# A recommender's attention over 200 history positions: three of 128 tiles per position fetched row by row, two by SyncE and one by ScalarE, instead of four

## The chip, the cores and the metric

The kernel runs on one core of one Trainium2 chip. The metric is the device time of one execution in microseconds (us). Engines are named as in the profile: PE is TensorE (PEld its weight loads), DVE is VectorE, ACT is ScalarE, POOL is GpSimd and SP is SyncE; a name with q is the queue of DMA issues and control instructions of that engine.

## What is computed

Of the reference, this is what matters (B = 16,384 users, L = 200 history positions, D = 64 values in a row, tables of 100,000 rows for items and users):

```python
def dice(x, alpha, axis):
    mean = jnp.mean(x, axis=axis, keepdims=True)
    var = jnp.var(x, axis=axis, keepdims=True)
    p = jax.nn.sigmoid((x - mean) * jax.lax.rsqrt(var + EPS))
    return x * (p + alpha * (1.0 - p))

u = u_emb[user]
it = i_emb[item]
c = c_emb[cate]
h = i_emb[hist]                      # 200 x 16384 rows of 64
itb = jnp.broadcast_to(it[None], h.shape)
feat = jnp.concatenate([h, itb, h - itb, h * itb], axis=-1)
a = dice(feat @ au_W1 + au_b1, au_alpha, axis=1)
w = a @ au_W2 + au_b2
cur = jnp.sum(w * jax.lax.stop_gradient(h), axis=0)
z = jnp.concatenate([u, it, c, cur], axis=-1)
z = dice(z @ W1 + b1, alpha1, axis=0)
z = dice(z @ W2 + b2, alpha2, axis=0)
return z @ W3 + b3
```

For each history position l, 16,384 rows are fetched from the item table at random indices. A small layer of 36 hidden values runs on each, is normalised over the 16,384 users of that l, and gives one weight per row; the weighted rows are summed over l. A head of three layers follows once.

## The kernel before

**Tiles and steps.** A tile is 128 rows. One l has 128 tiles, cut into eight chunks (c = 0 to 7) of sixteen tiles. One chunk is one step k (c = k % 8, l = k // 8), and there are 1,600 steps. Positions 0 to 179 run in a hardware loop of four passes of 45 l (LPB, line 19); the last 20 l and the head are written out behind it. The order of the instructions on each engine is written by hand, in `step` (line 368).

**Fetching.** `fetch` (304) writes the sixteen tiles of a chunk into one of five row buffers (128 x 16 x 64). POOL does it with one indirect DMA per tile (`gather`, 124; the call is line 125): 128 row indices lie in SBUF, one per partition, and each picks a row of 256 bytes. Chunks in SIDES = (1, 3, 5, 7) have only fifteen gathers; their sixteenth tile comes "by address". For it the indices, times the row length, lie as a list of integers in one partition (`load_addresses`, `scale_addresses`); an engine loads eight or sixteen of them into registers and issues one plain DMA of 256 bytes for each row (`addresses`, 267). For chunks 1 and 5 SP issues these (`rows_by_sync`, 275, asked for by `ask`, 398, 32 rows in each step), into one of three `side` buffers. For chunks 3 and 7 ACT issues them (`rows_by_scalar`, 285, in groups of eight, four groups in each step, split by `scalar_rows`, 403, into two slots of the step), into one of three `aside` buffers, with a semaphore for each (`landed`) on which ACT itself waits (`await_rows_by_scalar`, 295) for all 128 rows.

**One step, engine by engine.** The numbers are lags: step k fetches chunk k, transposes chunk k - 1, finishes the hidden layer of chunk k - 2 and weighs chunk k - 10, whose l has its mean and variance by then.

- `gate(k - 10)` (310): ACT writes p = sigmoid of the normalised hidden values into PSUM (pg).
- `weights(k - 10)` (314): DVE multiplies pg by the hidden values x into y; PE sums over the hidden values into wb, as blk_x times x plus blk_p times y. blk_x holds alpha times W2, blk_p holds (1 - alpha) times W2.
- `scalar_rows` slot 0, then `hidden(k - 2)` (322, ACT: px plus bias into x), `measure(k - 2)` (325, DVE: statistics of x), then `scalar_rows` slot 1.
- `turn(k - 1)` (330): in chunks of SIDES, ACT copies the tile that came by address into the row buffer (line 339); DVE transposes the buffer into hT (four instructions, line 154); PE multiplies hT by a unit matrix into ph in PSUM, and then begins px with blk_h times hT and blk_i times the item values.
- `weigh(k - 10)` (318, DVE): the weights times hT of chunk k - 10, added to the running sums.
- `product(k - 1)` (344): DVE multiplies ph by the item values into hm; PE adds blk_m times hm to px.
- `moments` (348), once per l: mean, variance, scale and shift; ACT takes a square root (168).

All matmuls but the head's second layer go through one helper, so they stand at line 159.

Of the kernel before, what the change touches and what calls it, by code (L numbers as in the profile page):

```python
# [9 lines left out]
I32 = mybir.dt.int32  # L10
AF = mybir.ActivationFunctionType
ALU = mybir.AluOpType
PSUM = bass.MemoryType.PSUM

P = 128
# [3 lines left out]
S = 32  # L19
CD = 2 * CH  # L20
LPB = 45
ROWS = 5
LAG = 10
XR = 9
IDX = 3
BY_SP = (1, 5)
BY_ACT = (3, 7)
SIDES = (1, 3, 5, 7)
LOAD = 16
GROUP = 8  # L30
ROW = 4 * D
U8 = mybir.dt.uint8
# [3 lines left out]
def din_kernel(  # L36
# [24 lines left out]
    nc = tc.nc  # L61
    L, B = r_hist.shape
    NT = B // P
    TD = 2 * CD // P
    ND = NT // TD
# [3 lines left out]
    ZA = P // 2  # L69
    ZB = Z1 - ZA  # L70
    NS = len(SIDES)
    NB, NA = len(BY_SP), len(BY_ACT)
    serial = iter(range(10**6))
    NC = NT - NS
    BODY = L - L % LPB if L > LPB else 0
    STATS = nc.vector.BN_STATS_DIM
# [5 lines left out]
    def make(name, *shape, dt=F32):  # L82
        return const.tile(list(shape), dt, name=name)
# [4 lines left out]
    def quarter(e, g, n=S):  # L88
        return slice((2 * e + g) * S, (2 * e + g) * S + n)
# [11 lines left out]
    ph = psum.tile([P, CD], F32, name="ph")  # L101
    pg = psum.tile([P, CD], F32, name="pg")
    wb = psum.tile([P, CD], F32, name="wb")

    rows = [make(f"rows{i}", P, TD, D) for i in range(ROWS)]
    hT = [make(f"hT{i}", P, CD) for i in range(LAG)]
    xs = [make(f"xs{i}", P, CD) for i in range(XR)]
# [3 lines left out]
    y = make("y", P, CD)  # L111
# [3 lines left out]
    side = [make(f"side{i}", P, D) for i in range(3)]  # L115
    aside = [make(f"aside{i}", P, D) for i in range(3)]
    landed = [tc.alloc_semaphore(f"landed{i}") for i in range(3)]
    addrs = make("addrs", 2 * S + 1, NS * P, dt=I32)
    addr = [addrs[i * S : i * S + 1] for i in range(3)]
    stats = [make(f"st{i}", P, 2 * ND, STATS) for i in range(3)]  # L120
    rstds = [make(f"rs{i}", P, 1) for i in range(3)]
    shifts = [make(f"sh{i}", P, 1) for i in range(3)]
# [33 lines left out]
    def layer(dst, pairs, first=True, last=True):  # L156
        for i in range(2):
            for j, (lhsT, rhs) in enumerate(pairs):
                nc.tensor.matmul(  # L159
                    dst[:, ts(i, CH)], lhsT, rhs[:, ts(i, CH)],  # L160
                    start=(first and j == 0), stop=(last and j == len(pairs) - 1),
                    skip_group_check=not (first and last),
                )
# [9 lines left out]
    blk_h = make("blk_h", P, P)  # L173
    blk_i = make("blk_i", P, P)
    blk_m = make("blk_m", P, P)
    blk_p = make("blk_p", P, P)
    blk_x = make("blk_x", P, P)
    unit = make("unit", P, P)
    au_w = make("au_w", P, 4, A)
    au_bias = make("au_bias", P, 1)  # L180
    au_al = make("au_al", P, 1)
# [4 lines left out]

    def attention_weights():
        nc.vector.memset(eps, EPS)
        for t in (blk_h, blk_i, blk_m, blk_p, au_bias, au_al, au_w2):
            nc.vector.memset(t, 0.0)  # L190
        nc.sync.dma_start(au_bias2, au_b2.partition_broadcast(P))
        for e in range(2):
            w = au_W1.rearrange("(g d) a -> d g a", d=D)[e * S : (e + 1) * S]
            for g in range(2):
                r = quarter(e, g)
                nc.sync.dma_start(au_w[r], w)
                for q, (a0, n) in enumerate(halves):
                    c, a = quarter(q, g, n), slice(a0, a0 + n)
                    nc.vector.tensor_add(blk_h[r, c], au_w[r, 0, a], au_w[r, 2, a])
                    nc.vector.tensor_sub(blk_i[r, c], au_w[r, 1, a], au_w[r, 2, a])  # L200
                    nc.vector.tensor_copy(blk_m[r, c], au_w[r, 3, a])
                    nc.vector.memset(blk_p[r, quarter(q, g)], 1.0)
        for g in range(2):
            for q, (a0, n) in enumerate(halves):
                r, a = quarter(q, g, n), slice(a0, a0 + n)
                nc.sync.dma_start(au_bias[r], col(au_b1)[a])
                nc.sync.dma_start(au_al[r], col(au_alpha)[a])
                nc.sync.dma_start(au_w2[r], au_W2[a])
        nc.vector.tensor_scalar(au_1al, au_al, -1.0, 1.0, ALU.mult, ALU.add)
        nc.vector.tensor_mul(au_1al, au_1al, au_w2)  # L210
        nc.vector.tensor_mul(au_al, au_al, au_w2)
        nc.vector.tensor_scalar_mul(blk_x, blk_p, au_al)
        nc.vector.tensor_scalar_mul(blk_p, blk_p, au_1al)
        nc.vector.tensor_copy(unit, lanes)
        nc.vector.tensor_single_scalar(unit, unit, float(P), ALU.is_equal)


    w1a = make("w1a", P, 4, P)
# [56 lines left out]
    def rows_by_sync(m, part, n):  # L275
        l, j = divmod(m, NB)
        s, dst = SIDES.index(BY_SP[j]), side[m % 3].bitcast(U8)
        for p0 in range(part * n, part * n + n, LOAD):
            for j, row in enumerate(addresses(l, s, p0, LOAD, mybir.EngineType.SP)):
                nc.sync.dma_start(dst[p0 + j : p0 + j + 1], row)  # L280


    keys = {}

    def rows_by_scalar(m, part):
        l, j = divmod(m, NA)
        s, dst = SIDES.index(BY_ACT[j]), aside[m % 3].bitcast(U8)
        key = keys.setdefault(m, f"rows{next(serial)}")
        for j, row in enumerate(addresses(l, s, part * GROUP, GROUP, mybir.EngineType.Activation)):
            p = part * GROUP + j  # L290
            dma = nc.scalar.dma_start(dst[p : p + 1], row).then_inc(landed[m % 3], 16)  # L291
            tc.no_tile_sem_insts.add(dma.ins.name)
            tc.add_to_no_dep_group(key, dma.ins)

    def await_rows_by_scalar(m):
        if m in keys:
            fence = nc.scalar.wait_ge(landed[m % 3], 16 * P)
            tc.declare_fence(fence.ins, group=keys.pop(m))
            nc.scalar.sem_clear(landed[m % 3])

    def has_side(k):
        return k % ND in SIDES
# [7 lines left out]
    def gate(k):  # L310
        i = k // ND % 3
        nc.scalar.activation(pg, xs[k % XR], AF.Sigmoid, bias=shifts[i], scale=rstds[i])  # L312

    def weights(k):
        nc.vector.tensor_mul(y, pg, xs[k % XR])  # L315
        layer(wb, [(blk_x, xs[k % XR]), (blk_p, y)])

    def weigh(k):
        nc.vector.scalar_tensor_tensor(wb, wb, au_bias2, hT[k % LAG], ALU.add, ALU.mult)  # L319
# [10 lines left out]
    def turn(k):  # L330
        if has_side(k):
            l, c = divmod(k, ND)
            if c in BY_ACT:
                m = l * NA + BY_ACT.index(c)
                await_rows_by_scalar(m)
                of = aside[m % 3]
            else:
                of = side[(l * NB + BY_SP.index(c)) % 3]
            nc.scalar.copy(rows[k % ROWS][:, TD - 1], of)  # L339
        transpose(hT[k % LAG], rows[k % ROWS])  # L340
        layer(ph, [(unit, hT[k % LAG])])
        layer(px, [(blk_h, hT[k % LAG]), (blk_i, itT[k % ND])], last=False)

    def product(k):
        nc.vector.tensor_mul(hm, ph, itT[k % ND])  # L345
# [47 lines left out]

    AHEAD = ND // NB - 1 - BY_SP[0]

    def ask(k, end):
        m, part = divmod(k + 1 + AHEAD, ND // NB)
        if m < end * NB:  # L400
            rows_by_sync(m, part, P * NB // ND)

    def scalar_rows(k, slot):
        m, part = divmod(k, ND // NA)
        n = P * NA // ND // GROUP
        for i in range(n)[slot::2]:
            rows_by_scalar(m, part * n + i)

    def steps(l0, n, end):
        for k in range(n * ND):  # L410
# [10 lines left out]
    with tc.manual_schedule():  # L421
        load_ids(ids[0], r_item)
        load_hist_ids(0, 0)
        load_addresses(0, 0)
        load_ids(ids[1], r_cate)
        load_ids(ids[2], r_user)
        nc.gpsimd.iota(lanes, pattern=[[1, P]], base=P, channel_multiplier=-1)
        attention_weights()
        for t in (*hT, *xs, *side, *aside, hm):
            nc.vector.memset(t, 0.0)  # L430
        for t in curT:
            nc.vector.memset(t, 0.0)
        for i in range(3):
            nc.vector.memset(rstds[i], 0.0)
            nc.vector.memset(shifts[i], 0.0)
        nc.vector.bn_stats(stats[-1 % 3][:, 0, :], hm[:, :CH])
        for c in range(1, 2 * ND):
            nc.vector.tensor_copy(stats[-1 % 3][:, c, :], stats[-1 % 3][:, 0, :])
        scale_addresses(0)
        layer(px, [(blk_m, hm)])  # L440

        for c in range(ND + 1):
            if c < ND:
                for n in range(TD):
                    j = column(c, n)
                    gather(rows[c % ROWS], ids[0][:, j : j + 1], n, i_emb)
            if c:
                transpose(itT[c - 1], rows[(c - 1) % ROWS])
        nc.vector.memset(rows[-1 % ROWS], 0.0)
        for k in range(-1 - AHEAD, 0):  # L450
            ask(k, L)
        head_weights()

    if BODY:
        with tc.For_i(0, BODY, LPB) as l0:  # L455
            with tc.manual_schedule():
                steps(l0, LPB, LPB + 1)
                await_rows_by_scalar(LPB * NA - 1)

    K = (L - BODY) * ND  # L460
    za = [hT[(K - LAG + c) % LAG] for c in range(ND)]
# [140 lines left out]
```

## Time and profile before

| | us |
|---|---|
| three executions | 31,616.96, 31,644.94, 31,647.4 |
| median | 31,644.94 |
| the profiled execution | 31,616.96 |
| its span, first to last instruction | 31,615.1 |
| mean granted TensorE clock | 0.810 |
| instructions | 357,535 |

The span is what the profile's shares refer to; the execution's own time is 1.9 us longer. In the profile's groups, a row gives line, engine, operation, output and inputs, the count, the busy time with the mean duration in ns, and the idle time of the engine just before, with what ended most of it. In a timeline, a row gives start, duration, engine, line, operation and, in brackets, the idle time before and what ended it; "issue" means that the engine waited for nothing that the profile shows. DMA issues and register work are not counted as busy.

### The profile page before, as it was taken

To read this page: it belongs to the slowest core of one execution; us is meant where nothing else is said; L and a number is where in the kernel's file an instruction comes from. 1 tells how busy PE (TensorE), PEld (TensorE's weight loads), DVE (VectorE), ACT (ScalarE), POOL (GpSimd) and SP (SyncE) were. 2 spreads that over 40 slices of the span, in tenths; PEclk is the share of its full clock that TensorE was granted. 3 is DMA by queue.
4 is the path that set the end of the run, shared out by engine and by line. 5 is a ranking of instruction groups with operands and counts; after the bars stand their busy time and mean duration, and the time that the engine had idled before them with its cause. 6 is when DMAs were issued, how large, how long until landed. Compare 5 with 4: busy or idle time off the path is not lost. (4 is left out here: it accounts for less than half of the span.)

```text
span 31615.1 us, 357535 instructions
## 1 busy us (share of the span) xinstructions
PE 20448.2 (65%) x38864; PEld 8357.2 (26%) x38864; DVE 15015.4 (47%) x18963; ACT 4479.6 (14%) x4670; POOL 23766.1 (75%) x25189
## 2 busy tenths in 40 slices
PE   5666666666666666666666666666666666666666
PEld 2222222222222222222222222222222222222222
DVE  4444444444444444444444444444444444444443
ACT  1111111111111111111111111111111111111111
POOL 7777777777777777777777777777777777777776
PEclk7888888888888888888888888888888888888887
DMA  1111111111111111111111111111111111111111
GB/s 29 28 28 28 28 28 28 28 28 28 28 28 28 28 28 28 28 28 28 28 28 28 28 28 28 28 28 28 28 28 28 28 28 28 28 28 28 28 28 23
DMA packets 1050292, 890.26 MB, mean 28 GB/s; under 512 B 644640, under 2 KB 644640, under 8 KB 1047784
## 3 DMA queue, kind: packets, MB, share of 16 engines
q0 software_dynamic: 805888, 826.84, 11.8%
q1 hardware_dynamic: 138920, 27.05, 0.4%
q10 hardware_dynamic: 102976, 13.32, 0.3%
q14 instruction: 2202, 18.04, 0.2%
q8 instruction: 306, 5.01, 0.1%
HBM read 865.03 MB, written 0.13 MB: 27 GB/s over the span
## 5 line engine op out<-in xcount | busy, mean ns | idle before, releaser
L125 POOL DMA_INDIRECT rows<-in_L_rec_i_emb,idx x24800 | 23403.2, 944 | 7593.5 <-issue 7032.1
L159 PE MATMUL ph<-hT,unit 128*128 128x512 f32 x6404 | 5658.4, 1029 | 10498.9 <-DVE hT L154 10498.9
L154 DVE STREAM_TRANSPOSE hT<-rows 64x512 f32<-64x512 f32 x6404 | 4518.8, 706 | 8256.8 <-DMA rows<-in_L_rec_i_emb,idx 4150.3
L328 DVE BATCH_NORM_STATS2 st<-xs 128x6 f32<-128x512 f32 x3204 | 2060.4, 685 | 7172.9 <-ACT xs L323 7172.9
L159 PEld LDWEIGHTS ph<-hT,unit 128*128 128x128 f32 x6404 | 1688.5, 295 | 13506.4 <-DVE hT L154 13334.4
L159 PE MATMUL px<-hT,blk_h 128*128 128x512 f32 x6404 | 3936.6, 702 | 0.0
L323 ACT ACTIVATE xs<-px,au_bias 128x1024 f32<-128x1024 f32 x1602 | 1784.3, 1114 | 14626.1 <-PE px L159 12323.9
L159 PE MATMUL wb<-y,blk_p 128*128 128x512 f32 x6440 | 3329.8, 599 | 455.3 <-DVE y L315 455.3
L159 PE MATMUL px<-itT,blk_i 128*128 128x512 f32 x6404 | 3368.8, 608 | 0.0
L159 PE MATMUL wb<-xs,blk_x 128*128 128x512 f32 x6440 | 3307.3, 595 | 51.5 <-PEq L455 39.9
L159 PE MATMUL px<-hm,blk_m 128*128 128x512 f32 x6408 | 3013.0, 592 | 40.5 <-DVE hm L430 40.5
L312 ACT ACTIVATE pg<-xs,sh,rs 128x1024 f32<-128x1024 f32 x1610 | 1939.8, 1205 | 3751.2 <-issue 2579.9
L315 DVE TENSOR_TENSOR y<-pg,xs 128x1024 f32<-128x1024 f32 x1610 | 1956.6, 1215 | 512.9 <-ACT pg L312 508.6
L159 PEld LDWEIGHTS px<-hT,blk_h 128*128 128x128 f32 x6404 | 1566.7, 245 | 2295.1 <-issue 2294.6
L319 DVE SCALAR_TENSOR_TENSOR wb<-wb,au_bias,hT 128x1024 f32<-128x1024 f32 x1610 | 2080.5, 1292 | 88.2 <-PE wb L159 36.0
L320 DVE TENSOR_TENSOR curT<-wb,curT 128x1024 f32<-128x1024 f32 x1610 | 1970.8, 1224 | 54.8
L345 DVE TENSOR_TENSOR hm<-ph,itT 128x1024 f32<-128x1024 f32 x1601 | 1941.2, 1212 | 0.0
L159 PEld LDWEIGHTS px<-itT,blk_i 128*128 128x128 f32 x6404 | 1374.9, 215 | 1925.3 <-issue 1925.3
L159 PEld LDWEIGHTS wb<-y,blk_p 128*128 128x128 f32 x6440 | 1212.0, 191 | 2081.7 <-issue 1445.9
L159 PEld LDWEIGHTS wb<-xs,blk_x 128*128 128x128 f32 x6440 | 1228.3, 191 | 1603.9 <-issue 1597.9
L159 PEld LDWEIGHTS px<-hm,blk_m 128*128 128x128 f32 x6408 | 1218.1, 190 | 1573.0 <-issue 1424.7
L339 ACT COPY rows<-aside 128x64 f32<-128x64 f32 x401 | 97.9, 244 | 2659.6 <-DMA aside<-in_L_rec_i_emb 2525.7
(155 smaller groups left out, 2171.5 us busy)
## 6 DMA issues: line engine op xcount, KB each, us to landing
aside<-in_L_rec_i_emb ACTq DMA_DIRECT2D x51200, 0.2 KB
side<-in_L_rec_i_emb SPq DMA_DIRECT2D x51200, 0.2 KB
rows<-in_L_rec_i_emb,idx POOLq DMA_INDIRECT x24800, 2.4
idx<-in_r_hist SPq DMA_DIRECT2D x200, 62.0 KB
addrs<-in_r_hist SPq DMA_DIRECT2D x200, 2.0 KB
rows<-in_L_rec_i_emb,ids POOLq DMA_INDIRECT x128, 2.4
rows<-in_L_rec_c_emb,ids POOLq DMA_INDIRECT x128, 2.4
rows<-in_L_rec_u_emb,ids POOLq DMA_INDIRECT x128, 2.4
```

Of the source, the lines that this page charges most:

```text
L125: nc.gpsimd.indirect_dma_start(out=dst[:, n, :], out_offset=None, in_=table, in_offset=bass.IndirectOffsetOnAxis(ap=ids, axis=0),)
L154: nc.vector.transpose(by_tile(dst[ts(e, D)], i), of[ts(i, D), :, ts(e, S)])
L159: nc.tensor.matmul(dst[:, ts(i, CH)], lhsT, rhs[:, ts(i, CH)], start=(first and j == 0), stop=(last and j == len(pairs) - 1), skip_group_c ...
L312: nc.scalar.activation(pg, xs[k % XR], AF.Sigmoid, bias=shifts[i], scale=rstds[i])
L315: nc.vector.tensor_mul(y, pg, xs[k % XR])
L319: nc.vector.scalar_tensor_tensor(wb, wb, au_bias2, hT[k % LAG], ALU.add, ALU.mult)
L320: nc.vector.tensor_add(curT[k % ND], wb, curT[k % ND])
L323: nc.scalar.activation(xs[k % XR], px, AF.Identity, bias=au_bias)
L328: nc.vector.bn_stats(stats[l % 3][:, 2 * c + i, :], xs[k % XR][:, ts(i, CH)])
L339: nc.scalar.copy(rows[k % ROWS][:, TD - 1], of)
L345: nc.vector.tensor_mul(hm, ph, itT[k % ND])
```

## The change

Three things are different.

1. SIDES becomes (3, 6, 7): three tiles of each l come by address and 125 by gathers. SP issues those of chunks 3 and 7, still 32 rows per step; ACT issues the one of chunk 6, in sixteen groups of eight spread over the steps c = 0 to 6, and waits for them in step c = 7.
2. The copy of hT into ph is an ACT instruction; the unit matrix and its matmul are gone.
3. ACT applies the factors to pg in PSUM (scale (1 - alpha) times W2, bias alpha times W2); PE then sums y alone, with a matrix of ones in blocks (blk_w).

```diff
-BY_SP = (1, 5)
-BY_ACT = (3, 7)
-SIDES = (1, 3, 5, 7)
+BY_SP = (3, 7)
+BY_ACT = 6
+SIDES = (3, 6, 7)
...
-    addrs = make("addrs", 2 * S + 1, NS * P, dt=I32)
-    addr = [addrs[i * S : i * S + 1] for i in range(3)]
+    addr = [make(f"addr{i}", 1, NS * P, dt=I32) for i in range(3)]
...
-                    nc.vector.memset(blk_p[r, quarter(q, g)], 1.0)
+                    nc.vector.memset(blk_w[r, quarter(q, g)], 1.0)
...
-        nc.vector.tensor_scalar_mul(blk_x, blk_p, au_al)
-        nc.vector.tensor_scalar_mul(blk_p, blk_p, au_1al)
-        nc.vector.tensor_copy(unit, lanes)
-        nc.vector.tensor_single_scalar(unit, unit, float(P), ALU.is_equal)
...
-    def await_rows_by_scalar(m):
-        if m in keys:
-            fence = nc.scalar.wait_ge(landed[m % 3], 16 * P)
-            tc.declare_fence(fence.ins, group=keys.pop(m))
-            nc.scalar.sem_clear(landed[m % 3])
+    def take_rows_by_scalar(l):
+        fence = nc.scalar.wait_ge(landed[l % 3], 16 * P)
+        tc.declare_fence(fence.ins, group=open_group.pop(l))
+        nc.scalar.sem_clear(landed[l % 3])
+        return aside[l % 3]
...
         nc.scalar.activation(pg, xs[k % XR], AF.Sigmoid, bias=shifts[i], scale=rstds[i])
+        nc.scalar.activation(pg, pg, AF.Identity, bias=au_al, scale=au_1al)
...
-        layer(wb, [(blk_x, xs[k % XR]), (blk_p, y)])
+        layer(wb, [(blk_w, y)])
...
         transpose(hT[k % LAG], rows[k % ROWS])
-        layer(ph, [(unit, hT[k % LAG])])
         layer(px, [(blk_h, hT[k % LAG]), (blk_i, itT[k % ND])], last=False)
+        nc.scalar.copy(ph, hT[k % LAG])
...
-    AHEAD = ND // NB - 1 - BY_SP[0]
+    PER = ND // NB

     def ask(k, end):
-        m, part = divmod(k + 1 + AHEAD, ND // NB)
+        m, part = divmod(k + 1, PER)
         if m < end * NB:
-            rows_by_sync(m, part, P * NB // ND)
+            rows_by_sync(m, part, P // PER)

     def scalar_rows(k, slot):
-        m, part = divmod(k, ND // NA)
-        n = P * NA // ND // GROUP
-        for i in range(n)[slot::2]:
-            rows_by_scalar(m, part * n + i)
+        l, c = divmod(k, ND)
+        if c > BY_ACT:
+            return
+        n = P // GROUP
+        mine = range(c * n // (BY_ACT + 1), (c + 1) * n // (BY_ACT + 1))
+        for part in mine[slot::2]:
+            rows_by_scalar(l, part)
...
-        for k in range(-1 - AHEAD, 0):
-            ask(k, L)
+        ask(-1, L)
...
-                await_rows_by_scalar(LPB * NA - 1)
```

More of the change, by code (lines that the diff above doesn't have):

```diff
@@ L71, in din_kernel @@
     NS = len(SIDES)
-    NB, NA = len(BY_SP), len(BY_ACT)
-    serial = iter(range(10**6))
+    NB = len(BY_SP)
     NC = NT - NS
@@ L175, in din_kernel @@
     blk_m = make("blk_m", P, P)
-    blk_p = make("blk_p", P, P)
-    blk_x = make("blk_x", P, P)
-    unit = make("unit", P, P)
+    blk_w = make("blk_w", P, P)
     au_w = make("au_w", P, 4, A)
@@ L188, in attention_weights @@
         nc.vector.memset(eps, EPS)
-        for t in (blk_h, blk_i, blk_m, blk_p, au_bias, au_al, au_w2):
+        for t in (blk_h, blk_i, blk_m, blk_w, au_bias, au_al, au_w2):
             nc.vector.memset(t, 0.0)
@@ L280, in rows_by_sync, with rows_by_scalar @@
                 nc.sync.dma_start(dst[p0 + j : p0 + j + 1], row)
[L283 to L288, printed above, removed]
+    groups = iter(range(10**6))
+    open_group = {}
+    def rows_by_scalar(l, part):
+        s, dst = SIDES.index(BY_ACT), aside[l % 3].bitcast(U8)
+        key = open_group.setdefault(l, f"rows{next(groups)}")
         for j, row in enumerate(addresses(l, s, part * GROUP, GROUP, mybir.EngineType.Activation)):
             p = part * GROUP + j
-            dma = nc.scalar.dma_start(dst[p : p + 1], row).then_inc(landed[m % 3], 16)
+            dma = nc.scalar.dma_start(dst[p : p + 1], row).then_inc(landed[l % 3], 16)
             tc.no_tile_sem_insts.add(dma.ins.name)
             tc.add_to_no_dep_group(key, dma.ins)
-    def await_rows_by_scalar(m):
-        if m in keys:
-            fence = nc.scalar.wait_ge(landed[m % 3], 16 * P)
-            tc.declare_fence(fence.ins, group=keys.pop(m))
-            nc.scalar.sem_clear(landed[m % 3])
+    def take_rows_by_scalar(l):
[3 more added lines that the diff above has]
+        return aside[l % 3]
     def has_side(k):
@@ L332, in turn @@
             l, c = divmod(k, ND)
[L333 to L336, printed above, removed]
+            if c == BY_ACT and l >= 0:
+                of = take_rows_by_scalar(l)
+            elif c == BY_ACT:
+                of = aside[l % 3]
             else:
```

## The prediction

> **What bounds the kernel now.** I read the page's first two parts, then its costliest groups, then POOL's timeline at four places of the run, and the chain and the waits last. The clock row holds 0.8 in nearly every slice (the mean granted clock is 0.810) and all 40 slices look alike, so one step can stand for all.
>
> ```profile
> span 31615.1 us, 357535 instructions
> PE 20448.2 (65%) x38864; PEld 8357.2 (26%) x38864; DVE 15015.4 (47%) x18963; ACT 4479.6 (14%) x4670; POOL 23766.1 (75%) x25189
> ...
> L125 POOL DMA_INDIRECT rows<-in_L_rec_i_emb,idx x24800 | 23403.2, 944 | 7593.5 <-issue 7032.1
> ```
>
> POOL is the busiest engine, and all but five of its instructions are gathers. Its idle time is 7593.5 over 24,800 gathers, 0.306 us each, and nearly all of it is "issue": nothing in the profile was waited for. A busy share of 75% hides that the engine is full, which its timeline shows: at the loop's first return, in the loop, and in the head after the last l, where no single rows are fetched.
>
> ```profile
> 7129.46 0.94 POOL L125 DMA_INDIRECT rows<-in_L_rec_i_emb,idx  x1 [0.30 <-issue]
> 7139.70 0.94 POOL L125 DMA_INDIRECT rows<-in_L_rec_i_emb,idx  x1 [9.30 <-issue]
> ...
> 15003.08 0.94 POOL L125 DMA_INDIRECT rows<-in_L_rec_i_emb,idx  x1 [0.30 <-issue]
> 15004.33 0.94 POOL L125 DMA_INDIRECT rows<-in_L_rec_i_emb,idx  x1 [0.31 <-issue]
> 15005.57 0.94 POOL L125 DMA_INDIRECT rows<-in_L_rec_i_emb,idx  x1 [0.30 <-issue]
> ...
> 31476.60 0.94 POOL L125 DMA_INDIRECT rows<-in_L_rec_u_emb,ids  x1 [0.30 <-issue]
> 31477.85 0.94 POOL L125 DMA_INDIRECT rows<-in_L_rec_u_emb,ids  x1 [0.30 <-issue]
> ```
>
> A gather starts every 1.25 us everywhere. The exact period comes from two loop returns: the first gathers after them start at 7139.70 and 14115.34, with 5,580 gathers from one to the other (45 l of 124) and an idle of 7.51 before the second. (6975.64 - 7.51 + 0.30) / 5,580 = **1.2488 us**. The whole run then adds up. 25,184 gathers (24,800 and 3 x 128) at 1.2488 are 31,449.8; the four long gaps (9.30, 7.51, 7.51 and 2.96 at the loop's returns and exit, less 0.30 each) are 26.1; the first gather starts at 2.86; from the end of the last (31478.79) to the end of the span are 136.3. The sum is 31,615.1, the span. So nothing but POOL sets the time, save that tail. The other engines wait for it: of the waits,
>
> ```profile
> DVE hT L154 <- DMA rows<-in_L_rec_i_emb,idx: 4150.3, 753, 7.8
> DVE hT L154 <- ACT rows L339: 3143.2, 579, 6.5
> ...
> ACT rows L339 <- DMA aside<-in_L_rec_i_emb: 2525.7, 395, 6.8
> ```
>
> the transposes wait for a gather's landing, or for ScalarE's small copy, which itself waits for rows. POOL fills one of five row buffers while the one before it is transposed, so three more are free: the others may fall some three steps (58 us) behind before POOL has to wait for a buffer. Where POOL's own waits name a releaser (a landing 1,797 times, 548.0 us, is the largest), each is 0.3 long, the standing gap. The chain that ended last, followed back over the last tenth of the span, is POOL 7%, issue 2% and DMA 1%: the same gathers and gaps.
>
> **The change, part by part.** *Gathers.* Per l, four tiles came by address and 124 by gathers; now it is three and 125. The listing of the changed program agrees: 65 more gathers in the 65 l that it spells out. Over 200 l that is 200 gathers more x 1.2488 = **+249.8 us**, all on the engine that sets the end. The three gathers of 128 tiles for item, category and user stay.
>
> *ScalarE's rows.* 51,200 row DMAs become 25,600. The sixteen issues in a timeline row take 6.27 us with their loads of addresses, 0.39 each. Per l ScalarE now has eight gates (1.205), eight hidden outputs (1.114), four copies (0.244), two table loads (1.283), a root (0.3) and 256 x 0.39 of issues: 9.6 + 8.9 + 1.0 + 2.6 + 0.3 + 99.8 = 122 us of the 155 that an l takes. The change takes 50 away and gains nothing, because ScalarE is hidden by POOL.
>
> *Two new ScalarE instructions a step.* The affine step on pg in PSUM and the copy of hT into ph are not in the trace. The nearest rows are L323 (128x1024, PSUM in, 1.114) and L312 (128x1024, PSUM out, 1.205). Below, each could take 1.1; above, twice L312, 2.4, if the affine step must first let the gate drain. I take 1.2 each, by L312, which writes the same memory: 16 x 1.2 = 19 per l, so ScalarE holds 122 - 50 + 19 = 91 of 156 us (110 with 2.4). Cost on the path at either end: 0.
>
> *TensorE.* Gone are 6,404 matmuls ph<-hT,unit (5658.4 us) and 6,440 wb<-xs,blk_x (3307.3): 20,448 falls to about 11,480. TensorE was not on the path, so this gains 0. VectorE's product, which read a ph written by TensorE, now waits for ScalarE's copy; what is queued behind that copy on ScalarE is the next step's gate.
>
> Where a step's latency could count is the loop of waits from one step to the next: hidden output 1.11, two statistics 1.28, four transposes 2.88, the ph copy 1.2, then on ScalarE the next gate and affine step 2.4 and the issues ahead of the next hidden output, 6.3 where the new split puts two groups there (c = 3 and 6) and 3.1 elsewhere. That is 15.2 us at worst and 12.0 else. POOL's step is 15.625 x 1.2488 = 19.5 us. The other branch, after the transposes weigh 1.29 + 1.22, product 1.21 and px's last matmuls 1.9, is 10.9 in all. The cover is 4.3 us at the worst step; if it were gone, each us over 19.5 in all steps would cost 1,600 us.
>
> The trace shows how matmuls run after an idle stretch: the first ph matmul of a step, now gone, takes 1.029 us in the mean, while those later in the burst take 0.59. Now px<-hT,blk_h comes first and may take 1.03 in place of 0.70; the eight matmuls left cost at most 8.2 us of 19.5, and the sum does not change. [...]
>
> *Waits and queues.* ScalarE's wait for landed rows comes once per l instead of twice, at c = 7, a step with no issues of its own; its last rows are issued a step earlier. SP issues 256 rows per l as before, 32 per step at 0.41 (12.09 us for 32 in a timeline row) of 19.5; the tiles are now c = 3 and 7 and the last quarter is still asked for two steps ahead. Before the loop it asks for one quarter instead of three, and has four steps to the first use. The address row is 384 long instead of 512: at most 0.45 us of VectorE per l, hidden. POOL's gathers wait for ScalarE's copy once per l less, in its queue, under 0.94 us of running gather: 0.
>
> *The loop's returns and exit.* Their gaps (26.1 us) are not worked out by any row. Below, they could vanish (-26.1); above, each could be the longest seen (4 x 9.0 = 36, +9.9). The last step's work ends at 7125.1 and the last gather at 7130.4, so POOL is last there too, and that stays: I take 0. The tail of 136.3 us is the head's own chain, which loses one small output DMA: 0.
>
> **Sum.** +249.8. Against the profiled execution (31,616.96, which is 1.9 over its span) this makes 31,866.8. That execution was the fastest of the three shown, 28.0 below their median, 31,644.94; from the median it is 31,894.7. Two of three executions lay at the higher place, so I say 31,890.
>
> **Rivals.**
>
> 1. *Gathers get cheaper.* If the 0.306 us between gathers were a wait for something that the row DMAs use, taking 25,600 of them away would shorten it. With 25,384 gathers, it ends level with before at 249.8 / 25,384 = 9.8 ns per gather, and faster beyond: at 20 ns, 31,645 + 250 - 508 = 31,387. Against it: in the first 160 us and in the head the gap reads 0.30 too, though no single rows move in the head. From 31379.23 to 31477.85 are 79 periods, 1.2483 each. So taking all rows away gained 0.5 ns, worth 13 us, not 250. Chance 0.05 for a gain of over 7.3 ns, where the time comes within 63 us of before.
>
> 2. *ScalarE becomes the bound.* It now stands between transposes and product. For it: the new copy is in the loop of waits, and two instruction forms have no row. Against it: 15.2 of 19.5 us. If the two cost 2.5 us each and issues ran a third slower, the worst steps (two of eight) would be 20 us; 400 steps x 0.5 = 200 more, about 32,095. Chance 0.04.
>
> 3. *The change does not add a gather*, since a tile is moved and not removed: then 31,645. The count of the listing speaks against it; chance 0.01.
>
> **How the numbers follow.** Forecast 0.90, rival 1 0.05, rival 2 0.04, rival 3 0.01. The range takes the forecast with its bounds: from the profiled execution, 31,866.8 - 26.1 = 31,841; from the median, 31,894.7 + 9.9 = 31,905 and some 25 for the spread of executions (30 us among the three shown): 31,840 to 31,930. That holds 0.88 or so, and no rival need be reached. About 0.2% is what a measurement of this kernel can tell from no change: 63 us. Forecast and rival 2 are slower: 0.94; rival 3 and half of rival 1 are within: 0.03; the rest is faster: 0.03.
>
> **What would show it.** Right: 25,000 gathers at L123 of the new file with mean 944 and 1.249 from start to start; POOL's idle near 0.306 each; ScalarE's issues halved; TensorE near 11,500 busy; gaps at the returns of 3 to 9 us. Wrong: a POOL wait named after ScalarE or VectorE with long idle times (rival 2), or a gap below 0.296 (rival 1).

## The result and the profile after

| | before | changed |
|---|---|---|
| median of four executions | 31,645.52 | 31,890.28 |
| lowest and highest | 31,616.96 to 31,647.4 | 31,864.21 to 31,894.12 |
| the profiled execution | 31,616.96 | 31,864.21 |
| its span | 31,615.1 | 31,862.4 |

The changed kernel is slower by 0.8%: ratio 1.0078, 95% interval 1.006 to 1.0095. The prediction was 31,890, with a range of 31,840 to 31,930.

The page of the changed kernel, its first lines and the groups that answer to those of before (after the bar: busy time and mean ns of one; then the idle time before them and what ended it):

```profile
span 31862.4 us, 279674 instructions
...
PE 15641.2 (49%) x26020; PEld 6235.8 (20%) x26020; DVE 14956.3 (47%) x18959; ACT 7911.4 (25%) x7681; POOL 23951.3 (75%) x25389
...
L123 POOL DMA_INDIRECT rows<-in_L_rec_i_emb,idx x25000 | 23588.4, 944 | 7656.7 <-issue 7249.9
L157 PE MATMUL px<-hT,blk_h 128*128 128x512 f32 x6404 | 5643.4, 980 | 14802.3 <-DVE hT L152 14802.3
...
L335 ACT COPY ph<-hT 128x1024 f32<-128x1024 f32 x1601 | 1627.3, 1016 | 15569.4 <-DVE hT L152 15560.5
...
L157 PE MATMUL px<-itT,blk_i 128*128 128x512 f32 x6404 | 4724.9, 831 | 0.0
...
L305 ACT ACTIVATE pg<-pg,au_al,au_1al 128x1024 f32<-128x1024 f32 x1610 | 1895.2, 1177 | 54.1
```

There are 200 gathers more and each is what it was: 944 ns, with 7656.7 / 25,000 = 0.306 us idle before it, again "issue". 77,861 instructions have gone, TensorE is 4,807 us less busy, and the kernel is 247.3 us longer in its span. The timeline of POOL in the changed kernel, around the loop's first return, at its second return, and inside the loop (start, duration, in brackets the idle time before):

```profile
7184.52 0.94 POOL L123 DMA_INDIRECT rows<-in_L_rec_i_emb,idx  x1 [0.30 <-issue]
7189.95 0.94 POOL L123 DMA_INDIRECT rows<-in_L_rec_i_emb,idx  x1 [4.49 <-issue]
...
14223.87 0.94 POOL L123 DMA_INDIRECT rows<-in_L_rec_i_emb,idx  x1 [11.19 <-issue]
...
15003.11 0.94 POOL L123 DMA_INDIRECT rows<-in_L_rec_i_emb,idx  x1 [0.31 <-issue]
15004.35 0.94 POOL L123 DMA_INDIRECT rows<-in_L_rec_i_emb,idx  x1 [0.30 <-issue]
```

The same sum as before, from the first return to the second: 45 l are now 5,625 gathers, and (14223.87 - 7189.95 - 11.19 + 0.30) / 5,625 = 1.2485 us from start to start. The span's increase comes apart as follows.

| term | us |
|---|---|
| 25,384 gathers x 1.24854, less 31,449.8 of before | +243.1 |
| of it, 200 gathers more, at 1.2488 | +249.8 |
| of it, each gather 0.26 ns cheaper | -6.7 |
| gaps at the three returns and the exit: 4.49, 11.19, 11.19, 5.36 (less 0.30 each: 31.0, for 26.1) | +4.9 |
| behind the last gather: 135.3 for 136.3 | -1.0 |
| sum | +247.0 |

The span grew by 247.3. The three corrections add to less than 3 us. The gap of 5.36 at the exit is the only one of the four behind which the profile names a releaser (a queued instruction of ScalarE, ACTq L260); in the run with the tiles alone, below, the gap there is 5.4 too, behind a load of indices.

The waits of the changed kernel (engine, line, what is waited for; us in total, times, longest):

```profile
ACT ph L335 <- DVE hT L152: 15560.5, 1600, 13.4
...
DVE hT L152 <- DMA rows<-in_L_rec_i_emb,idx: 9110.0, 1419, 9.1
POOL rows L123 <- issue: 7359.6, 24043, 11.2
```

ScalarE's new copy is always there first: it waits for the transposes in each of the 1,600 steps, 9.7 us in the mean, and these wait for the landing of a gather 1,419 times (753 before). POOL's idle time is its standing gap, as before.

### The profile page after: what moved, and what is told of

Same layout as the page of the kernel before. It is cut to its first block, busy times and chain, and to the rows that moved or that the text cites. A ratio compares the mean times of both kernels' runs of the same rounds, so it can differ in the third digit from the quotient of the medians.

```text
span 31862.4 us, 279674 instructions
## 1 busy us (share of the span) xinstructions
PE 15641.2 (49%) x26020; PEld 6235.8 (20%) x26020; DVE 14956.3 (47%) x18959; ACT 7911.4 (25%) x7681; POOL 23951.3 (75%) x25389
## 5 line engine op out<-in xcount | busy, mean ns | idle before, releaser
L123 POOL DMA_INDIRECT rows<-in_L_rec_i_emb,idx x25000 | 23588.4, 944 | 7656.7 <-issue 7249.9
L157 PE MATMUL px<-hT,blk_h 128*128 128x512 f32 x6404 | 5643.4, 980 | 14802.3 <-DVE hT L152 14802.3
L335 ACT COPY ph<-hT 128x1024 f32<-128x1024 f32 x1601 | 1627.3, 1016 | 15569.4 <-DVE hT L152 15560.5
L157 PEld LDWEIGHTS px<-hT,blk_h 128*128 128x128 f32 x6404 | 1809.1, 313 | 17816.4 <-issue 17000.6
L157 PE MATMUL px<-itT,blk_i 128*128 128x512 f32 x6404 | 4724.9, 831 | 0.0
L157 PE MATMUL wb<-y,blk_w 128*128 128x512 f32 x6440 | 3414.4, 657 | 1257.1 <-DVE y L308 1242.5
L157 PEld LDWEIGHTS px<-itT,blk_i 128*128 128x128 f32 x6404 | 1857.3, 290 | 2850.8 <-issue 2850.8
L305 ACT ACTIVATE pg<-pg,au_al,au_1al 128x1024 f32<-128x1024 f32 x1610 | 1895.2, 1177 | 54.1
L157 PEld LDWEIGHTS wb<-y,blk_w 128*128 128x128 f32 x6440 | 1307.3, 207 | 2988.8 <-issue 1537.7
L332 ACT COPY rows<-side 128x64 f32<-128x64 f32 x401 | 97.9, 244 | 1237.6 <-DMA side<-in_L_rec_i_emb 1085.1
```

The costliest lines, as they stand in the source:

```text
L123: nc.gpsimd.indirect_dma_start(out=dst[:, n, :], out_offset=None, in_=table, in_offset=bass.IndirectOffsetOnAxis(ap=ids, axis=0),)
L157: nc.tensor.matmul(dst[:, ts(i, CH)], lhsT, rhs[:, ts(i, CH)], start=(first and j == 0), stop=(last and j == len(pairs) - 1), skip_group_c ...
L305: nc.scalar.activation(pg, pg, AF.Identity, bias=au_al, scale=au_1al)
L335: nc.scalar.copy(ph, hT[k % LAG])
```

## The experiments

In the first four runs and their set the kernel before took 31,677.58 (31,674.88 to 31,680.15, 13 executions). In three later sets, each on another chip, the kernel before itself took 49,022 to 49,101 in the median, half as long again. A run of those is read only beside the kernel before of its own set, and its total does not test the sum above.

### 1. The tiles alone

The changed kernel with parts 2 and 3 of the change undone:

```diff
-    addr = [make(f"addr{i}", 1, NS * P, dt=I32) for i in range(3)]
+    addrs = make("addrs", 2 * S + 1, NS * P, dt=I32)
+    addr = [addrs[i * S : i * S + 1] for i in range(3)]
...
-        nc.scalar.activation(pg, pg, AF.Identity, bias=au_al, scale=au_1al)
...
-        layer(wb, [(blk_w, y)])
+        layer(wb, [(blk_x, xs[k % XR]), (blk_p, y)])
...
+        layer(ph, [(unit, hT[k % LAG])])
...
-        nc.scalar.copy(ph, hT[k % LAG])
```

> The tiles alone: three tiles by address as in the changed kernel, while ph and the factors of pg stay on TensorE as before. Theory (POOL's gathers alone set the time): 25,000 gathers, +250 us, so within 10 us of the changed kernel, near 31,890 in the median and 1.248 to 1.249 us from gather to gather. Rival (the moves to ScalarE carry part of the difference, for better or worse): the time is off the changed kernel's by that part, more than 60 us if it is to matter.

Measured: 31,922.81 (31,864.49 to 31,924.53), ratio 1.0077, interval 1.006 to 1.0094. Two lines of its page:

```profile
span 31862.7 us, 302145 instructions
...
L124 POOL DMA_INDIRECT rows<-in_L_rec_i_emb,idx x25000 | 23588.6, 944 | 7657.3 <-issue 7246.1
```

The whole loss is there with the 12,844 matmuls back in place, and the span is within 0.3 us of the changed kernel's. So the gathers carry it, and the moves between engines give nothing back. The median lies 33 us over the 31,890 that was expected, and that of the kernel before in this set 32 over its earlier one; the difference within the set is 245, near the 250 expected.

### 2. The engines alone

The kernel before with parts 2 and 3 only (its four tiles stay):

```diff
+        nc.scalar.activation(pg, pg, AF.Identity, bias=au_al, scale=au_1al)
...
-        layer(wb, [(blk_x, xs[k % XR]), (blk_p, y)])
+        layer(wb, [(blk_w, y)])
...
-        layer(ph, [(unit, hT[k % LAG])])
...
+        nc.scalar.copy(ph, hT[k % LAG])
```

> The engine moves alone: four tiles by address as before, but ScalarE makes ph and applies the factors to pg. Theory (POOL alone): as before, 31,645 in the median, with TensorE's busy time lower by some 5,000 us for nothing. Rival (ScalarE becomes the bound): per l it now holds 32 groups of eight rows at 0.8 for the load of addresses and 8 x 0.338 for the issues, 112 us, and 8 x (1.203 + 1.113 + 1.177 + 1.016) = 36, and 4 for copies, table loads and the root: 152 of the 155 us that POOL takes. With a few waits in its queue it passes POOL, and the time rises by one or more per cent, over 32,000, with POOL idle in front of row buffers.

Measured: 31,677.11 (31,675.44 to 31,679.97), ratio 1.0000, interval 0.999 to 1.0009. From its page:

```profile
PE 15799.4 (50%) x26020; PEld 6183.3 (20%) x26020; DVE 15051.3 (48%) x18959; ACT 7985.0 (25%) x7881; POOL 23821.9 (75%) x25189
...
L125 POOL DMA_INDIRECT rows<-in_L_rec_i_emb,idx x24800 | 23458.3, 946 | 7597.8 <-issue 7085.1
```

and two of POOL's waits:

```profile
POOL rows L125 <- issue: 7196.4, 23486, 9.3
...
POOL rows L125 <- ACT xs L318: 8.9, 29, 0.3
```

TensorE's busy time fell by 4,649 us and the time by nothing. This kernel also puts the most on ScalarE: about 133 us of instructions and issues per l (worked out below) and 16 x 1.1 of the two new ones, some 151 of 155. Even so POOL does not wait for it: where its waits name ScalarE, as above, they are 0.3 long, the standing gap. A gather took 946 ns here, 944 in the profiles above; with its gap that is 2.4 ns on each of 25,184, or 60 us. That accounts for this execution's 31,677 beside the 31,617 of the first profile. The kernel with the tiles alone was profiled at 944 ns and 31,864, its lowest, and lay 58 us higher in the median; that a gather of 946 ns made its other executions longer is likely, but they have no profile.

### 3 and 4. Half of the gathers

Eight gathers per chunk instead of fifteen or sixteen, in the changed kernel and in the kernel before. Half of the history rows are left out. This takes POOL off the path and shows what lies under it.

```diff
-        for n in range(TD - has_side(k)):
+        for n in range(TD // 2):
```

> The changed kernel with eight gathers in each chunk instead of fifteen or sixteen; the other tiles of a chunk keep what the buffer held, so half of the history rows are left out. POOL's step would be 8 x 1.2486 = 10 us. Theory (the rest of a step has a cover of 4 to 7 us under the 19.5 of POOL): the loop of waits is the bound then, 12 to 15 us a step, 12.8 in the mean: near 21,000 us in all. Rival (the cover is larger than worked out, POOL still sets the time): near 16,500.

> The kernel before with eight gathers in each chunk; half of the history rows are left out. Theory: ScalarE's 256 row issues are the bound then, 112 us and 23 of other work per l, 135: near 27,400 us in all, which would show that the change bought about 30 us of cover per l that nothing uses. Rival (ScalarE overlaps its issues with its other work): nearer 22,000, as for the changed kernel.

Measured, one execution each: 22,452.51 and 28,552.59. The chain that ended last, from the page, and POOL's wait for transposes, from the waits; first of the changed kernel with half of the gathers, then of the kernel before with half:

```profile
SPq 8%; DVE 6%; issue 4%; PE 4%; POOL 4%; DMA 3%; ACT 2%; ACTq 2%; DVEq 0%; POOLq 0%
```

```profile
POOL rows L123 <- DVE hT L152: 5816.8, 1494, 8.3
```

```profile
ACTq 10%; PE 5%; DVE 5%; issue 4%; SPq 3%; POOL 2%; ACT 2%; DMA 2%; DVEq 0%; POOLq 0%
```

```profile
POOL rows L125 <- DVE hT L154: 12124.4, 1564, 15.6
```

Now POOL does wait for the transposes to free a row buffer. With the head and what comes before the loop (some 620 us: 384 gathers of 1.249, the first 3 and the last 135) taken off, 21,830 / 200 = 109.2 us per l are left in the changed kernel, 13.6 per step, and (28,552.6 - 620) / 200 = 139.7 per l before, 17.5 per step. Both floors were above what was expected (21,000 and 27,400). In both chains the issues of single rows lead, SyncE's in the changed kernel and ScalarE's in the kernel before; other engines' shares are not far below. SyncE's timeline in the changed kernel with half of the gathers:

```profile
15031.21 0.36 SPq L136 DMA_DIRECT2D idx<-in_r_hist  x1
15032.91 25.15 SPq L272 DMA_DIRECT2D side<-in_L_rec_i_emb  x64
...
15059.89 77.82 SPq L272 DMA_DIRECT2D side<-in_L_rec_i_emb  x192
15138.19 0.36 SPq L136 DMA_DIRECT2D idx<-in_r_hist  x1
```

From one load of indices to the next, one l, are 107 us, and SyncE issues in nearly all of it. With the loads of addresses (1.3 us ahead of the 64) a row takes (25.15 + 1.3) / 64 = 0.41 us, and 256 of them 106 us. In the kernel before, ScalarE's 133 us per l (worked out below) are most of the 139.7. So the change did something: it lifted the slack under POOL's step from 19.4 - 17.5 = 1.9 us to 19.5 - 13.6 = 5.9. Nothing collects that slack, since POOL's own step grew.

### 5. No rows by address

The changed kernel without any row DMA by SyncE or ScalarE: three of the 128 tiles of an l stay zero.

```diff
-        if m < end * NB:
-            rows_by_sync(m, part, P // PER)
+        return
...
-        if c > BY_ACT:
-            return
+        return
...
-            if c == BY_ACT and l >= 0:
-                of = take_rows_by_scalar(l)
-            elif c == BY_ACT:
+            if c == BY_ACT:
```

> The changed kernel without any row DMAs: SyncE and ScalarE issue none, and the three tiles of each l that came by address are zeros, so 3 of 128 history rows are left out. POOL's 25,384 gathers stay. Theory: the changed kernel's time, a ratio of 1.0078 to before, from gather to gather the same to 0.5 ns. Rival (the gap of 0.305 between gathers, or the gather itself, contends with row DMAs): shorter by over 2.5 ns per gather, a ratio under 1.0058.

Measured: 37,411.39, with the kernel before at 49,027.32 in that set; ratio 0.7634, interval 0.7612 to 0.7657. The gathers' group in its page, then POOL's timeline:

```profile
L123 POOL DMA_INDIRECT rows<-in_L_rec_i_emb,idx x25000 | 23610.6, 944 | 13084.4 <-issue 7442.6
```

```profile
15040.04 0.95 POOL L123 DMA_INDIRECT rows<-in_L_rec_i_emb,idx  x1 [0.30 <-issue]
15041.29 0.94 POOL L123 DMA_INDIRECT rows<-in_L_rec_i_emb,idx  x1 [0.30 <-issue]
15042.54 0.95 POOL L123 DMA_INDIRECT rows<-in_L_rec_i_emb,idx  x1 [0.30 <-issue]
```

The total says nothing here, but the pitch does: with no row DMA in the whole program, a gather still follows the last after 1.25 us. Over all pairs of gathers with only the standing gap between them, the mean in the trace is 1.2491 us, and 1.2486 in the changed kernel's first profile: 0.5 ns longer, where the rival needed 2.5 ns less. The standing gap of 0.30 is not a wait for the queues that the row DMAs use. Rival 1 (cheaper gathers) falls.

### 6. Gathers of 64 rows

The changed kernel with indirect DMAs on 64 partitions instead of 128. Half of the gathered rows are left out.

```diff
-            out=dst[:, n, :],
+            out=dst[: ids.shape[0], n, :],
...
-            gather(rows[k % ROWS], idx[l % IDX][:, j : j + 1], n, i_emb)
+            gather(rows[k % ROWS], idx[l % IDX][: P // 2, j : j + 1], n, i_emb)
```

> The changed kernel with its 25,000 gathers on 64 partitions instead of 128; half of the history rows are left out, the count of gathers stays. Theory A (a gather is paid per instruction): 944 and 0.305 stay, near 31,880. Theory B (paid per row): 472 and 0.305, 12.1 us a step, under the 13.65 that the rest of a step takes, so near 22,500. Between the two the time tells the fixed part.

Measured, one execution in the set where the kernel before took 49,027.32: 47,310.39. The gather in its page:

```profile
L123 POOL DMA_INDIRECT rows<-in_L_rec_i_emb,idx x25000 | 22514.1, 901 | 24042.5 <-DVE hT L152 16354.7
```

The totals that were expected were for a kernel before of some 31,650 and can't be compared; the gather's own time can. Half the rows save 43 of 944 ns. Between 64 and 128 rows a gather's price is nearly all per instruction, so it is their number that counts and not the rows they fetch.

### 7 to 12. Fewer tiles, more tiles, and the changed kernel again

Two tiles by address per l, both by SyncE, in the changed kernel (126 gathers per l):

```diff
-BY_ACT = 6
-SIDES = (3, 6, 7)
+BY_ACT = 8
+SIDES = (3, 7)
...
-        if c > BY_ACT:
+        if BY_ACT not in SIDES or c > BY_ACT:
```

> The changed kernel with only the two tiles that SyncE fetches by address; ScalarE issues no rows, and 126 tiles of each l are gathers. Theory (a gather costs its period on POOL, whatever the other engines do): 400 gathers more than before at 1.249, +500 us or a ratio of 1.0158. Rival (the row DMAs slow the gathers): with 51,200 of them gone the period falls by at least the 2.5 ns per gather that could be seen, and the ratio stays under 1.0138.

> Two tiles by address, 126 gathers per l, once more. Theory: a ratio of 1.0158 where the kernel before takes some 31,650. On a chip like that of the run ahead: 0.95 again.

> Two tiles of rows per l instead of four, none issued by ScalarE: 126 gathers per l, 25,200 in the loop, 200 more than the changed kernel and 400 more than the kernel before within the resolution of the tiles. Where the kernel before takes some 31,650 us, the theory that the gathers alone set the time gives +400 x 1.2488 = +500 us against the kernel before, ratio 1.016 (1.014 to 1.018): a straight line through four, three and two tiles. The rival, that the third tile cost something of its own beside its gathers (its groups of eight, its semaphores), gives less than 1.2488 us per gather and a ratio nearer 1.008. If the kernel before takes about 49,000 us here, the ratio is near 0.95 again and tells nothing of this.

A fifth tile, by SyncE, in every other l, in the kernel before (meant as a version faster than both: 100 gathers fewer). SyncE then loads its addresses in groups of eight instead of sixteen, and a pass of the loop holds 90 l instead of 45:

```diff
-LPB = 45
+LPB = 90
...
-SIDES = (1, 3, 5, 7)
-LOAD = 16
+ODD = 6
+SIDES = (1, 3, 5, 6, 7)
+LOAD = 8
+AHEAD = 11
+TURNS = ((0, 1), (0, 5), (1, 1), (1, 5), (1, ODD))
...
-        return k % ND in SIDES
+        l, c = divmod(k, ND)
+        return c in SIDES and (c != ODD or l % 2 == 1)
...
+        for g in range(5 * k + AHEAD, 5 * k + AHEAD + 5):
+            m, part = divmod(g, P // LOAD)
+            if m >= 0 and m // 5 * 2 + TURNS[m % 5][0] < end:
+                rows_by_sync(m, part)
```

> The kernel before with a fifth tile by address in every other l (chunk 6), issued by SyncE, which then has 320 rows per l in the mean instead of 256, in groups of eight; the loop passes hold 90 l, so there are two returns fewer. Theory (a gather is worth its period, and the other engines have room): 100 gathers fewer x 1.249 = -125 us, and some -15 us for the two returns, near 31,505 or a ratio of 0.9956. SyncE's rows would take 320 x 0.43 = 138 us of 154 per l, and ScalarE its 140. Rival (SyncE becomes the bound, with waits in its queue that the sum leaves out): the same or slower, and the row copies wait for landings.

> The kernel before with a fifth tile of rows, issued by SyncE, in every other l: 100 gathers fewer (25,089 on POOL for 25,189). If the kernel before takes some 31,650 us on this chip, the theory that the gathers alone set the time gives 100 x 1.2488 us = 125 us less, ratio 0.996 (0.994 to 0.998). The rival is that SyncE, with 320 row issues per l on average (x 0.416 us = 133 us of 155) and 384 in the l's that have five (160 us of 154), holds POOL up: ratio 1.00 to 1.03. If the kernel before takes about 49,000 us here, as on two of the chips, the number of instructions decides and the ratio is near 1.10 again.

And the changed kernel as it is, in such a set:

> The changed kernel once more, beside runs of the kernel before on this chip. Theory (POOL's gathers alone): a ratio of 1.0078 wherever the kernel before takes some 31,650. On a chip where the kernel before takes some 49,000, as in the three runs that went ahead, gathers do not set the time; there the changed kernel, with 78,000 instructions fewer, would be the faster one by several per cent.

Measured; "per l" is the time over 200:

| kernel | time, before of its set | ratio, interval | rows by SP, ACT per l | instructions | us per l |
|---|---|---|---|---|---|
| no rows (run 5) | 37,411.39, 49,027.32 | 0.7634, 0.7612 to 0.7657 | 0, 0 | 116,705 | 187 |
| two tiles | 46,569.22, 49,027.32 | 0.9498, 0.9472 to 0.9525 | 256, 0 | 224,467 | 233 |
| two tiles, again | 46,574.08, 49,022.55 | 0.9507, 0.9481 to 0.9533 | 256, 0 | 224,467 | 233 |
| two tiles, a third time | 46,613.57, 49,101.46 | 0.9502, 0.9476 to 0.9528 | 256, 0 | 224,467 | 233 |
| changed | 47,343.09, 49,022.55 | 0.9661, 0.9636 to 0.9687 | 256, 128 | 279,674 | 237 |
| before | 49,022.55 | 1 | 256, 256 | 357,535 | 245 |
| fifth tile in every other l | 54,103.3, 49,022.55 | 1.1044, 1.1019 to 1.1069 | 320, 256 | 388,444 | 271 |
| the same, a second time | 54,188.15, 49,101.46 | 1.1043, 1.1015 to 1.1072 | 320, 256 | 388,444 | 271 |

All of these missed the sum by gathers, in both directions, and the change is faster than before in such a set (0.9661). Four expectations reckoned with such a set (two tiles again and a third time, the fifth tile a second time, the changed kernel), from the runs ahead of them, and there they held: 0.95, 1.10, and faster by some per cent. The profile says why the sum does not apply: POOL is no longer full, busy for 51% of the span in the changed kernel run again and for 75% in its first profile. Of the changed kernel run again, its waits:

```profile
POOL rows L123 <- DVE hT L152: 14982.5, 924, 45.4
ACT xs L316 <- issue: 13351.0, 1271, 44.2
ACT rows L332 <- DMA side<-in_L_rec_i_emb: 13056.0, 393, 43.1
```

and SyncE's timeline over 250 us, first in the changed kernel's first profile (an l of 156 us), then in the one run again (start, length of the stretch of issues, their number):

```profile
15087.40 25.18 SPq L272 DMA_DIRECT2D side<-in_L_rec_i_emb  x64
15112.91 0.23 SPq L141 DMA_DIRECT2D addr<-in_r_hist  x1
15114.57 127.44 SPq L272 DMA_DIRECT2D side<-in_L_rec_i_emb  x192
```

```profile
15003.49 164.50 SPq L272 DMA_DIRECT2D side<-in_L_rec_i_emb  x192
15177.09 0.01 SPq L136 DMA_DIRECT2D idx<-in_r_hist  x1
15181.99 56.44 SPq L272 DMA_DIRECT2D side<-in_L_rec_i_emb  x64
```

A stretch of 64 rows takes 56.44 us where it took 25.18, 0.88 us per row for 0.39 (the long stretch of the first profile has waits for buffers in it). The gathers themselves take 946 ns with 0.30 between them; POOL stands still 14,982.5 us for transposes. These wait for ScalarE's copies (9,161 us), and the copies for SyncE's rows. What is slow are small instructions of the queues: between 10,000 and 20,000 us of the span, a register move on ScalarE takes 29 ns from the 10th to the 99th percentile in the first profile, and in this one 30% of them took 700 ns or so (SyncE: 19%; of their DMA issues, 30% and 19% above 600, none before), while activations (1,130 ns in the mean), transposes (706 and 703) and gathers hardly changed.

The same trace shows when they are slow. Of the register moves and row issues in that stretch that start more than 10 us into an unbroken run of gathers, 83% on SyncE and 69% on ScalarE take over 600 ns; in the first 5 us of such a run it is 5% and 4%, and when POOL has stood still for more than 2 us, 2% and 6%. So in this run the slow issues go together with the gathers. In the first profile they do not: there POOL gathers without a break and none is slow. That the gathers bring it about in such a set is likely from the order in time, but no run shows it.

Two readings of the table offer themselves. *The number of instructions decides*: their order in time follows it, but not the slope: from no rows to two tiles an instruction costs 9,158 us / 107,762 = 85 ns, from two tiles to three (774 / 55,207) 14 ns, from before to the fifth tile (5,081 / 30,909) 164 ns. *SyncE's rows are the floor*: 256 x 0.88 = 225 us per l stands close under the 233 to 245 of the three kernels with 256 rows. With the fifth tile the timeline of the second run has 240 rows in 195.71 us, 0.82 each, and 320 x 0.82 = 262 stands under 271. SyncE's queue itself waits 0.8 ms in all in the changed kernel run again, and 10.6 ms in its first profile: it no longer gets ahead. That fits better, but does not say all: without any rows an l still takes 187 us, where 125 gathers are 156. Why these instructions stretch is open. The packets of the instruction queue (q14 in the page) took 434 ns in the mean, for 430 in the first profile, so it is not their transfer that takes longer; what else it could be no run here tells. Open too, since these kernels ran in such sets alone, are the straight line through two tiles (expected 1.016) and whether the fifth tile in every other l is the faster version that the sum says (0.996).

## Why the prediction was right

*POOL bounds the kernel, and 200 gathers at 1.2488 set the change.* Right where the kernel before takes some 31,650 us, and shown from two sides: the tiles alone gave the ratio 1.0077, the engines alone 1.0000. The term of 249.8 measured +243.1 with the small change of the period, and the whole +247.3.

*The loop's returns and the exit, taken as 0 within -26.1 and +9.9.* They cost 4.9. The forecast of single gaps, 3 to 9 us, was too narrow: two are 11.19. At the three returns (4.49, 11.19 and 11.19) the profile names nothing that was waited for; what fills these gaps no run here shows.

*The profiled execution against the median.* 31,866.8 was expected for the profiled one and it took 31,864.21. That two of three executions of before lay higher is what made 31,890 of it; three of four lay at 31,890 to 31,894. That the median came within 0.3 us of it is luck: -6.7, +4.9 and -1.0 us were not forecast and nearly cancel, and executions of one kernel differ by 30 us here and by 60 with the tiles alone.

*ScalarE's two new instructions at 0.* Right. They measured 1.177 and 1.016 us, 1.2 was taken. A row's issue was estimated too low: 0.39 leaves out the load of addresses ahead of the first group. Issues are 0.338 apart, a load for eight takes 0.75, and (8 x 0.338 + 0.75) / 8 = 0.43. So ScalarE held about 133 us per l before and not 122, and holds some 95 now (7911.4 / 200 = 39.6 busy and 128 x 0.43 = 55), where 91 was expected. The loop of waits was put at 12.0 to 15.2 us per step; with half of the gathers the step is 13.6, which SyncE's issues nearly fill by themselves, so the loop was not measured alone. The 19.5 of POOL cover either.

*TensorE would fall to about 11,480.* Wrong: 15,641.2. Two lines of before answer to two shown above:

```profile
L159 PE MATMUL px<-hT,blk_h 128*128 128x512 f32 x6404 | 3936.6, 702 | 0.0
...
L159 PE MATMUL px<-itT,blk_i 128*128 128x512 f32 x6404 | 3368.8, 608 | 0.0
```

Two things were missed. The removed groups' times were subtracted from a busy time in which overlapping matmuls count once (the groups of before add to more than 22,600, where the engine was busy for 20,448; afterwards they add to 16,819 for 15,641, so 988 less overlaps). And the matmuls that stay got slower, more than allowed for: px from blk_h took 980 ns for 702, within the 1.03 foreseen, but px from blk_i 831 for 608 and wb 657 for 599. Together that is 1,707 + 1,356 + 85 us, and with the 988 and 23 of blk_m it makes up the 4,159 between forecast and result. The mean granted clock went from 0.810 with 24 matmuls a step to 0.721 with 16. The single runs tell what it goes with: with the tiles alone (24 matmuls a step) it was 0.812, with px from blk_h at 714 ns and from blk_i at 609, and with the engines alone (16) 0.727, with 979 and 830. So the slower matmuls came with the moves to ScalarE, which take eight matmuls out of a step, and not with the tiles; why the clock falls no run here shows. The 1.029 us that the prediction gives for the first ph matmul of a step is the mean of all four of a step. All of this had no effect on the time, as the prediction had it.

*The rivals.* Cheaper gathers: the period fell by 0.26 ns, of the 9.8 needed, and with no row DMA at all it is still 1.25. ScalarE as the bound: where POOL's waits name ScalarE they are 0.3 long, even where it has some 151 of 155 us to do; the one longer wait is the 5.36 at the changed kernel's exit. A change that adds no gather: 25,000 were counted.

## What to carry to other kernels

An engine busy for 75% can be the whole bound, as POOL was here with 0.944 us of gather and 0.30 of gap: add up its period, instruction plus standing gap, over the whole span, and if the sum meets the span, price a change by the instructions it puts on that engine and by nothing else. That holds as long as the engine is full: in the three later sets it was not (51% busy in the changed kernel), and in the one where both kernels ran the same change was a gain (ratio 0.9661). What is taken off the others is then only cover; removing POOL's work for one run (half of the gathers) shows how much cover there is and which engine is next, which the waits of the full kernel do not say. Here, fewer rows by address made room on the other engines (5.9 us under POOL's step, for 1.9) and added 243 us to the bound; unless that room is used to take more off the bound than was added, it is a loss. No run here shows such a use that pays.

## What the runs showed of the hardware

- An indirect DMA on POOL costs by the instruction: 944 ns for 128 rows and 901 for 64, and 0.30 us between two that nothing in the profile explains, with 102,400, 76,800 or no row DMAs in the program.
- The same gather takes 944 ns in some profiles and 946 in others, which with its gap is 60 us of such a kernel; executions of the kernel with the tiles alone differ by as much.
- One row DMA by address costs 0.41 us of SyncE (a load of sixteen addresses included) and 0.43 of ScalarE (a load of eight), both estimated from the timelines above.
- In three sets of runs the kernel before took half as long again, and in the profile of the changed kernel from one of them up to 30% of the register moves took 700 ns instead of 29, most of them while POOL gathered, with the work instructions nearly unchanged. In the set where both kernels ran their order turned round: the change was worth -3.4% instead of +0.8%. The cause was not found.
